# An attention and mixture-of-experts block on one Trainium2 core: the tiled order from pair 2 on, powers on GpSimd, and another split of transfers and scatters

## The chip, the core and the metric

The kernel runs on one core of a Trainium2 chip. The metric is the device time of one execution in microseconds, and the figure compared is the median of several runs. The names of the engines are those of the profile: PE is TensorE (matmuls; PEld is its weight load), DVE is VectorE, ACT is ScalarE, POOL is GpSimd, SP is SyncE, which here only issues transfers. Each engine executes its own instructions in program order. Transfers (DMA) are issued from SP, ACT or POOL.

## What is computed

The input is x with 8 batches of 512 tokens and 256 channels, all in float32. Cut to what matters, the reference is:

```python
xn = layernorm(x)                          # (x - mean) / sqrt(var + 1e-5), per token
# attention, 16 heads of 64, causal
kv = (xn @ w_kv_down) @ w_kv_up            # a latent of rank 128, then keys and values
k, v = kv[..., :1024], kv[..., 1024:]
att = softmax(causal((q @ k^T) * 64 ** -0.5))   # q = xn @ w_q
attn = (att @ v) @ w_out
# feed-forward: 8 experts, the best two per token, and one shared expert
scores = sigmoid(xn @ gate_w.T + lb_bias)
topw, topi = top_k(scores, 2); topw = topw / topw.sum()
for e in range(8):
    sel = (topi == e).any(-1)
    wmean = sum of e's weights / max(number of e's tokens, 1)
    out += where(sel, mlp_e(xn) * wmean, 0)  # mlp: silu(x @ g.T) * (x @ u.T) @ d.T
out += mlp_shared(xn)
result = x + attn + out
```

## The kernel before, in words

**Pairs.** The main loop (L906 and on) runs over 64 steps m, called pairs: 8 batches times 8 pairs of heads. For a pair, TensorE makes `ps_s`, the scores of two heads (`scores`, L615), for four blocks i of 128 query rows, against the 128 (i + 1) keys that causality leaves. VectorE adds the mask and takes the minimum of each row (L622; queries are scaled by a negative number), ScalarE takes the exponent with the row's sum (L629), and VectorE transposes the result in squares of 32 (`transposed`, L642 and L649) into `blk`. Sixteen transfers per pair (`moved`, L661) carry `blk` to `pt` across partitions, so that keys lie on partitions. Two pairs later `weighted` (L704) multiplies `pt` with the values into `ps_y`. The softmax's division comes last: `inverse_sums` (L678 to L683) takes the reciprocals of the row sums, transposes them, and POOL writes them to DRAM as `row`; `spread_sums` (L691) reads `row` back, spread over partitions, as `rb`, in two transfers from SP; ScalarE copies `ps_y` to `yT` (L716), and POOL multiplies it by `rb` (L717). The last pair alone is multiplied by VectorE straight from `ps_y` (L714). `project` (L729) takes the finished batch through `w_out`, with the shared expert's hidden rows.

**Two orders of a pair.** Up to pair 13 (`BLOCK0 = 14`) a pair is done in two halves: blocks (0, 3), then (1, 2), and a half's transposes come behind the next half's scores. From pair 14 on there is one block: scores (3, 1), two exponents, the transposes of block 3, `weighted` of the pair two before, scores (2, 0), two exponents, the transposes of block 1, and then the rest of the list below, at whose 0.65 mark the last transposes, `inverse_sums` and `moved` are emitted. In the old order `moved` of pair m comes at the start of pair m + 1, and `weighted` in the second half of pair m + 2.

**The list of other work.** `put(m, place, f, ...)` notes a piece of work for pair m at a place between 0 and 2; the loop emits a pair's pieces by place. `put_half` counts in half pairs. PE, DVE, ACT and SP keep the order in which instructions are emitted, and so does POOL from pair 0 on. Keys, queries and values of the next pair stand at 0.22 to 0.26.

**Layer norm.** Batch 0 is normalised before the loop (from L816 on: sixteen idle matmuls, then `statistics`, `deviations`, `normalise`, `turn`, then `queries`, `latent`, `keys`). The other batches come in pairs 0 to 10, one every five halves: `load_x` (L135), `statistics` (DVE, L256), `deviations` (DVE, L264 to L273: the reciprocal root by a starting guess on the bits and three Newton steps), `normalise` (POOL, L278), two `turn`s (PE transposes, L288, and an ACT copy), `logits` (L297) and `save_xnT`. In the same pairs POOL issues transfers that fill a DRAM buffer with zeros (L232), lay out the experts' weights (L224) and begin the sums (L244).

**Router, scatter, experts.** The router (L326 to L437) runs in pairs 11 to 13, mostly on VectorE. In pairs 14 to 21 each pair has four `scatter_rows` (L449), each two indirect transfers of 128 rows from POOL, which sort the tokens by expert. In these pairs `moved` gives one of its sixteen transfers to POOL and five to ACT, whose five are kept back until the next pair's block (`rest`); SP issues ten. In other pairs POOL has five and SP eleven. From pair 22 on `expert_fetch`, `expert_turn`, `expert_hidden`, `expert_down` and `expert_add` (L485 to L536) run for 39 tiles of 256 rows, spread over the half pairs up to pair 59.

Of the kernel before, what the change touches and what calls it, by code (L numbers as in the profile page):

```python
# [32 lines left out]
F32 = mybir.dt.float32  # L33
I32 = mybir.dt.int32
# [14 lines left out]
def kernel(  # L49
# [196 lines left out]

    mv = keep.tile([P, NTILE, 2], F32, name="mv")
    rstd = keep.tile([P, NTILE], F32, name="rstd")
    sc = keep.tile([P, NTILE, E], F32, name="sc")
    xnTs: dict = {}  # L250
    lats, qs, ks, vs, pts, rss, rbs, blks = {}, {}, {}, {}, {}, {}, {}, {}
# [4 lines left out]
        nc.vector.bn_stats(st, xins[n // NQ][:, n % NQ, :])  # L256
        nc.vector.bn_aggr(mv[:, n, :], st)

    def deviations(b):


        ve, y, z = (small.tile([P, NQ], F32, tag=f"dev{k}", name="dev") for k in range(3))
        half = small.tile([P, NQ], I32, name="half")
        nc.vector.tensor_scalar_add(ve, mv[:, ts(b, NQ), 1], 1e-5)  # L264
        nc.vector.tensor_single_scalar(half, ve.bitcast(I32), 1, op=ALU.logical_shift_right)
        nc.vector.tensor_scalar(
            y.bitcast(I32), half, -1.0, float(0x5F3759DF), ALU.mult, ALU.add
        )
        for k in range(3):
            nc.vector.tensor_mul(z, y, y)  # L270
            nc.vector.tensor_mul(z, z, ve)
            nc.vector.tensor_scalar(z, z, -0.5, 1.5, ALU.mult, ALU.add)
            nc.vector.tensor_mul(y if k < 2 else rstd[:, ts(b, NQ)], y, z)  # L273

    def normalise(b, by):
        for j in range(NQ):
            n = b * NQ + j
            by.tensor_scalar(  # L278
                xns[:, n, :C], xins[b][:, j, :], mv[:, n, 0:1], rstd[:, n : n + 1],
                ALU.subtract, ALU.mult,  # L280
            )

# [368 lines left out]
                    pr[:, j, nr * P :].rearrange("p (b k) -> p b k", k=QB),  # L651
                )

    def moved(b, p, by_pool, by_act=0):


        pt = ptp.tile([P, NB, 2, NBLK, QB], F32, name="pt")

        def begin(by, k):
            a, kb = divmod(k, NB)  # L660
            by.dma_start(pt[ts(kb, QB), a], blks[b, p][ts(a, QB), kb])  # L661

        left = []
        for k in range(NB * NB):
            if k * by_pool % 16 < by_pool:
                begin(nc.gpsimd, k)
            elif k % 3 == 1 and len(left) < by_act:
                left.append(k)
            else:
                begin(nc.sync, k)  # L670
        pts[b, p] = pt
        return lambda: [begin(nc.scalar, k) for k in left]

    def inverse_sums(b, p):


        ri, riT = ris[p % len(ris)]
        nc.vector.reciprocal(  # L678
            ri[:, : 2 * NQ], rss[b, p].rearrange("p j i -> p (j i)")
        )  # L680
        nc.vector.transpose(riT, ri)  # L681
        row = rowp.tile([NB, QB, QB], F32, name="row")
        nc.gpsimd.dma_start(row.rearrange("a x q -> (a x) q"), riT)  # L683
        rows[b, p] = row

    def spread_sums(b, p):

        rb = rbp.tile([P, NB, NQ * QB], F32, name="rb")
        for j in range(2):
            row = rows[b, p][:, ts(j, NQ), :].rearrange("a i q -> a (i q)")  # L690
            nc.sync.dma_start(  # L691
                rb[ts(j, D)], row.unsqueeze(0).broadcast_to([D, NB, NQ * QB])
            )
        rbs[b, p] = rb

    def weighted(b, p, final=False):


        ps = bank([P, NB, NQ, QB], "ps_y")
        for c in range(NQ):  # L700
            for j in range(2):
                h = 2 * p + j
                at = at_ci[c, c]
                nc.tensor.matmul(  # L704
                    ps[ts(j, D), :, c:, :],
                    vs[b, h // VH][:, c, ts(h % VH, D)],
                    pts[b, p][:, :, j, at : at + NQ - c, :],
                    start=(c == 0), stop=(c == NQ - 1),
                )
        yT = ytp.tile([P, T], F32, name="yT")  # L710
        y = yT.rearrange("p (i a q) -> p a i q", a=NB, q=QB)
        rb = rbs[b, p].rearrange("p a (i q) -> p a i q", q=QB)
        if final:
            nc.vector.tensor_tensor(y, ps, rb, ALU.mult)  # L714
        else:
            nc.scalar.copy(y, ps)  # L716
            nc.gpsimd.tensor_tensor(y, y, rb, ALU.mult)  # L717
        yTs[b, p] = yT
# [42 lines left out]


    EARLY, HALF = 0.3, 0.65
    BLOCK0 = 14
    plan: dict = {}

    def put(m, place, f, *a):
        if place >= 2:
            m, place = m + 1, place - 2
        plan.setdefault(m, []).append((place, len(plan[m]) if m in plan else 0, f, a))  # L770
# [44 lines left out]
    idle = bank([P, T], "ps_i")  # L815
    for k in range(8):  # L816
        nc.tensor.matmul(idle, ones, mask, start=True, stop=True)
    for n in range(NQ):
        statistics(n)
    deviations(0)  # L820
    normalise(0, nc.vector)
    xnTs[0] = xtp.tile([P, NCC, T], F32, name="xnT")
    for h in range(2):
        turn(0, h, xnTs[0])
    queries(0, 0)
    latent(0)
    keys(0, 0)
    put(0, 0.5, lambda: logits(0, xnTs[0]))

# [4 lines left out]
    def put_half(h, place, f, *a):  # L834
        put(h // 2, h % 2 + place, f, *a)
# [5 lines left out]
    for b in range(1, B):  # L841
        h = (b - 1) * LNH // 2
        if b > 2:
            put_half(h - 2, 0.5, load_x, b)
        for j in range(NQ):
            put_half(h + j // 2, 0.6, statistics, b * NQ + j)
        put_half(h + 2, 0.35, deviations, b)
        put_half(h + 2, 0.36, normalise, b, nc.gpsimd)
        put_half(h + 4, 0.1, start_turn, b)
        put_half(h + 5, 0.1, lambda b: turn(b, 1, lnT[b]), b)  # L850
        put_half(h + 6, 0.4, lambda b: (logits(b, lnT[b]), save_xnT(b, lnT[b])), b)
# [19 lines left out]
    for k in range(12):  # L871
        put(R0 + k // 4, 0.35 + 0.5 * (k % 4), lambda: next(steps, None))
    S0 = R0 + 3
    for n in range(NTILE):
        put(S0 + n // NQ, 0.35 + 0.5 * (n % NQ), scatter_rows, n)


    def begin_experts():
# [3 lines left out]
        ep = tmp_pools.enter_context(tc.tile_pool(name="ep", bufs=1))  # L882
        xouts = ep.tile([P, NQ, C], F32, name="xout")

    E0 = S0 + NTILE // NQ
    END = len(pairs) - 5
    put(E0, 0.1, begin_experts)
    first, n_halves = 2 * E0 + 5, 2 * (END - E0) - 7
# [9 lines left out]
        put_half(2 * END + b, 0.7, bring_out, b)  # L898
    put_half(2 * END + B - 1, 0.7, bring_back)

    scattering = range(S0, S0 + NTILE // NQ)
    ordered = ExitStack()
    last = []
    rest = []
    assert BLOCK0 <= S0
    for m in range(len(pairs) + 1):  # L906
        if m == 0:
            ordered.enter_context(tc.manual_schedule(engines={nc.gpsimd.engine}))
        todo = sorted(plan.pop(m, ()), key=lambda e: e[:2])
        for g, group in enumerate(((0, 3), (1, 2)) if m < BLOCK0 else ()):  # L910
            chunks, exps = scores(*pairs[m], group)
            for chunk in last:
                transposed(*chunk)
            last = chunks
            if g == 0 and m > 0:
                moved(*pairs[m - 1], 5)
            for e in exps[:2]:
                e()
            del exps[:2]
            for place, _, f, a in todo:  # L920
                if (place >= 1) == g:
                    if place - g > EARLY:
                        while exps:
                            exps.pop(0)()
                    f(*a)
                    if exps:
                        exps.pop(0)()
            while exps:
                exps.pop(0)()
        if m < BLOCK0:  # L930
            continue

        chunks, exps = [], []
        if m < len(pairs):
            chunks, exps = scores(*pairs[m], (3, 1))
            for chunk in last:
                transposed(*chunk)
            if last:
                moved(*pairs[m - 1], 5)
            last = []  # L940
            exps.pop(0)()
            exps.pop(0)()
            transposed(*chunks.pop(0))
            weighted(*products.pop(m))
            more = scores(*pairs[m], (2, 0))
            exps.pop(0)()
            exps.pop(0)()
            transposed(*chunks.pop(0))
            chunks, exps = more
        for f in rest:  # L950
            f()
        rest = []


        for place, _, f, a in todo + [(2, 0, lambda: None, ())]:
            if place > EARLY - 0.07:
                while exps:
                    exps.pop(0)()
            if place > HALF and chunks:
                while chunks:  # L960
                    transposed(*chunks.pop(0))
                inverse_sums(*pairs[m])
                if m in scattering:
                    rest = [moved(*pairs[m], 1, 5)]
                else:
                    moved(*pairs[m], 8 if m >= len(pairs) - 2 else 5)
            f(*a)
            if exps:
                exps.pop(0)()
# [3 lines left out]
    for tt in range(NQ):  # L973
        project(B - 1, tt, pss[tt], first=NS + NPAIR - 3, last=NS + NPAIR - 1)
    assert not plan and products.keys() == {len(pairs) + 1}, (plan, products)
    weighted(*pairs[-1], final=True)
    for tt in range(NQ):
        project(B - 1, tt, pss[tt], first=NS + NPAIR - 1)
    ordered.close()
# [45 lines left out]
```

## Time and profile before

| | |
|---|---|
| runs, median (lowest to highest) | 987.74 us (986.42 to 988.87), 3 runs |
| the profiled execution | 987.82 us; its span, first to last instruction, 986.1 us |
| mean granted TensorE clock | 0.978 |
| busy in the span | PE 933.2 us (95%), PEld 562.6, DVE 596.4, ACT 506.9, POOL 597.5 |
| transfers | 190.63 MB in 127594 packets; queue q1 (SP) 38.0% of 16 engines' span, q0 (POOL) 34.6% |

A busy share is a mean over stages that have different limits, so the profile is read by stage. "Granted clock" is the share of TensorE's full speed that the throttle gave. In the chain of waits each row is a start in us, a length in us, and the instruction, transfer or wait that held the end back at that moment; a name with q behind the engine (SPq, ACTq) is an instruction of the engine's queue, such as the issue of a transfer. In a timeline, the brackets hold the idle time in front of an instruction and what ended it.

### The profile page before, as it was taken

What the parts mean: (1) busy time and instruction counts of PE and PEld (TensorE: products, weight loads), DVE (VectorE), ACT (ScalarE), POOL (GpSimd) and SP (SyncE); (2) the same over time, 40 slices, a digit from 0 to 9 for tenths busy, and PEclk for the clock granted to TensorE, in tenths of its full rate; (3) what the DMA queues carried; (4) which work ended last, traced back from release to release, by engine and by line L of the source; (5) the groups of instructions that cost most, each with busy time, mean ns of one, the idle gap of its engine ahead of it and who ended that gap; (6) DMA issues with size and microseconds to landing.
All of it is one profiled execution on the core that took longest, in us unless ns stands there. A gap on an engine that the chain in (4) does not pass through costs nothing.

```text
span 986.1 us, 16151 instructions
## 1 busy us (share of the span) xinstructions
PE 933.2 (95%) x4326; PEld 562.6 (57%) x4326; DVE 596.4 (60%) x2160; ACT 506.9 (51%) x1468; POOL 597.5 (61%) x819
## 2 busy tenths in 40 slices
PE   8898999997679889999999999999999999999997
PEld 3454555643346435675666756576556775557555
DVE  3986783796543567446664456754567546674660
ACT  2564464544443456445664556644467544664550
POOL 2587676346677764646676566675757747665450
PEclk9899899999789999999999999999999999999999
DMA  7489788675566768867787677886778868767782
GB/s 263 124 267 307 239 280 279 169 213 170 167 185 165 203 169 227 206 148 160 197 195 204 164 164 190 209 207 157 166 181 209 202 152 193 184 151 155 194 238 79
DMA packets 127594, 190.63 MB, mean 193 GB/s; under 512 B 24896, under 2 KB 88640, under 8 KB 127264
## 3 DMA queue, kind: packets, MB, share of 16 engines
q1 hardware_dynamic: 88160, 104.28, 38.0%
q0 software_dynamic: 36864, 81.78, 34.6%
q10 hardware_dynamic: 2480, 3.55, 1.2%
q8 instruction: 35, 0.57, 0.3%
q14 instruction: 55, 0.45, 0.2%
HBM read 66.45 MB, written 50.18 MB: 118 GB/s over the span
## 4 chain that ended last, share of the span: by engine, by line
PE 76%; DMA 7%; DVE 5%; SPq 4%; ACT 3%; issue 2%; ACTq 1%; POOL 0%; another core or an unknown queue 0%; POOLq 0%; DVEq 0%
PE ps_s L615 14%; PE ps_o L729 13%; PE ps_y L704 13%; PE ps_q L587 9%; PE ps_e L512 7%; PE ps_k L578 5%; PE ps_v L568 4%; SPq L661 4%; PE ps_gu L470 3%; PE ps_ed L525 3%; DMA pt<-blk 3%; ACT pr L629 2%; PE ps_x L500 2%; PE ps_lg L297 1%; DMA rb<-row 1%
## 5 line engine op out<-in xcount | busy, mean ns | idle before, releaser
L622 DVE CUSTOM_DVE_ANT_0 ps_s<-ps_s,mask 128x128 f32<-128x128 f32 (+3 forms) x512 | 241.5, 516 | 207.9 <-PE ps_s L615 155.1
L629 ACT ACTIVATE pr<-ps_s,mn 128x128 f32<-128x128 f32 (+3 forms) x512 | 268.6, 534 | 152.8 <-DVE mn L622 125.7
L642 DVE STREAM_TRANSPOSE blk<-pr 128x384 f32<-128x384 f32 (+2 forms) x512 | 209.5, 449 | 24.6 <-ACT pr L629 15.5
L615 PE MATMUL ps_s<-k,q 64*128 64x512 f32 (+3 forms) x1024 | 189.3, 471 | 30.6 <-ACT q L592 20.8
L661 POOL DMA_DIRECT2D pt<-blk x294 | 156.4, 649 | 71.0 <-DVE ri L678 30.6
L536 POOL DMA_INDIRECT acc_d<-ye,to x78 | 127.5, 1635 | 93.5 <-issue 38.3
L704 PE MATMUL ps_y<-pt,v 128*64 128x512 f32 (+3 forms) x1024 | 157.6, 451 | 8.1 <-DVE th L462 4.2
L615 PEld LDWEIGHTS ps_s<-k,q 64*128 64x128 f32 x1024 | 92.0, 190 | 116.6 <-issue 52.5
L717 POOL TENSOR_TENSOR yT<-yT,rb 128x512 f32<-128x512 f32 x63 | 84.6, 1342 | 96.7 <-ACT yT L716 89.4
L704 PEld LDWEIGHTS ps_y<-pt,v 128*64 128x64 f32 x1024 | 70.2, 140 | 102.8 <-issue 82.9
L729 PE MATMUL ps_o<-wo_sb,yT 128*128 128x256 f32 x512 | 120.1, 380 | 2.3 <-POOL yT L717 1.5
L587 PE MATMUL ps_q<-xnT,wq_sb 128*128 128x512 f32 x256 | 121.0, 595 | 0.7 <-ACT xnT L291 0.7
L729 PEld LDWEIGHTS ps_o<-wo_sb,yT 128*128 128x128 f32 x512 | 96.9, 190 | 17.5 <-POOL yT L717 1.9
L629 ACT ACTIVATION_READ_ACCUMULATOR pr<-ps_s,mn 128x1 f32 x512 | 106.4, 208 | 0.0
L683 POOL DMA_DIRECT2D row<-riT x64 | 46.7, 729 | 58.4 <-DVE riT L681 47.7
L587 PEld LDWEIGHTS ps_q<-xnT,wq_sb 128*128 128x128 f32 x256 | 49.3, 193 | 55.5 <-issue 51.6
L512 PE MATMUL ps_e<-xgT,w 128*128 128x256 f32 x312 | 74.3, 381 | 0.1
L622 DVE DVE_READ_ACCUMULATOR2_ANT mn<- 128x1 f32 x512 | 72.6, 142 | 0.0
L449 POOL DMA_INDIRECT xg_d<-xn,at_i x64 | 62.9, 982 | 13.1 <-issue 13.1
L578 PE MATMUL ps_k<-lat,wkv_sb 128*128 128x512 f32 x128 | 69.8, 628 | 0.7 <-ACT lat L560 0.7
L512 PEld LDWEIGHTS ps_e<-xgT,w 128*128 128x128 f32 x312 | 58.7, 190 | 17.2 <-issue 5.8
L716 ACT COPY yT<-ps_y 128x512 f32<-128x512 f32 x63 | 37.1, 588 | 59.6 <-PE ps_y L704 44.1
(137 smaller groups left out, 1020.0 us busy)
## 6 DMA issues: line engine op xcount, KB each, us to landing
pt<-blk SPq DMA_DIRECT2D x690, 80.0 KB
pt<-blk POOLq DMA_DIRECT2D x294, 80.0 KB
rb<-row SPq DMA_DIRECT2D x128, 128.0 KB
xg_d<-zero POOLq DMA_DIRECT2D x26, 408.0 KB
xg<-xg_d SPq DMA_DIRECT2D x39, 272.0 KB
acc_d<-in_x_dram POOLq DMA_DIRECT2D x8, 512.0 KB
xin<-in_x_dram SPq DMA_DIRECT2D x7, 512.0 KB
xnT_d<-lnT SPq DMA_DIRECT2D x7, 512.0 KB
```

Source lines behind the costliest of these rows:

```text
L512: nc.tensor.matmul(ps[:, v, :], w[:, ds(at + cc * I, I)], turned[t][0][:, cc, :], start=(cc == 0), stop=(cc == NCC - 1),)
L536: nc.gpsimd.indirect_dma_start(out=acc_d[:, :], out_offset=bass.IndirectOffsetOnAxis(ap=turned[t][1][:, u : u + 1], axis=0), in_=results[t ...
L578: nc.tensor.matmul(ps, wkv_sb[:, ts(p, P)], lats[b], start=True, stop=True)
L587: nc.tensor.matmul(ps, wq_sb[:, cc, ts(p, P)], xnTs[b][:, cc, :], start=(cc == 0), stop=(cc == NCC - 1),)
L615: nc.tensor.matmul(pss[j][:, ds(at, n)], q[ts(j, D), ts(i, P)], k[ts(j, D), :n], start=True, stop=True,)
L622: nc.vector.tensor_tensor_reduce(out=pss[j][:, ds(at, n)], in0=pss[j][:, ds(at, n)], in1=mask[:, T - n :], scale=1.0, scalar=NO_MIN, op0=A ...
L629: nc.scalar.activation(o, s, AF.Exp, bias=mn, scale=-1.0, accum_out=rs[:, j, i : i + 1])
L642: nc.vector.transpose(blk[:, :, j, i : i + (nr - 1) * (NQ - 1) + 1 : NQ - 1, :].rearrange("p b c q -> p c b q"), pr[:, j, : nr * P].rearra ...
L661: by.dma_start(pt[ts(kb, QB), a], blks[b, p][ts(a, QB), kb])
L704: nc.tensor.matmul(ps[ts(j, D), :, c:, :], vs[b, h // VH][:, c, ts(h % VH, D)], pts[b, p][:, :, j, at : at + NQ - c, :], start=(c == 0), s ...
L717: nc.gpsimd.tensor_tensor(y, y, rb, ALU.mult)
L729: nc.tensor.matmul(ps, l[:, ts(tt, P)], r, start=(k == 0), stop=(k == len(ops) - 1))
```

## The change

It has six parts.

1. `BLOCK0` goes from 14 to 2: pairs 2 to 13 are emitted in the order that pairs 14 to 63 have already.
2. `deviations` becomes two POOL instructions, an addition and a power with exponent -0.5, in place of fifteen on DVE. `load_x` is placed half a pair earlier.
3. In the scatter pairs ACT issues no transfers: POOL issues two of the sixteen, SP fourteen. VectorE multiplies `ps_y` by `rb` in these pairs, so that ACT's copy and POOL's multiply go.
4. The 32 `scatter_rows` are shared over nine pairs, 14 to 22, as 3, 3, 3, 3, 5, 5, 4, 3, 3. The experts begin a pair later and end where they ended.
5. `row` is laid out so that a head's 512 values lie together, and `rb` comes in one transfer from SP in place of two. The order of its columns changes with it.
6. The prologue takes `deviations` and `normalise` in two halves and computes the latent before the queries.

```diff
+    exponent = const.tile([P, NQ], F32, name="exponent")
+    nc.gpsimd.memset(exponent, -0.5)
...
-    def deviations(b):
...
-        for k in range(3):
-            nc.vector.tensor_mul(z, y, y)
-            nc.vector.tensor_mul(z, z, ve)
-            nc.vector.tensor_scalar(z, z, -0.5, 1.5, ALU.mult, ALU.add)
-            nc.vector.tensor_mul(y if k < 2 else rstd[:, ts(b, NQ)], y, z)
+    def deviations(first, count):
+
+        r = rstd[:, ds(first, count)]
+        nc.gpsimd.tensor_scalar_add(r, mv[:, ds(first, count), 1], 1e-5)
+        nc.gpsimd.tensor_tensor(r, r, exponent[:, :count], ALU.pow)
...
-    def moved(b, p, by_pool, by_act=0):
+    def moved(b, p, by_pool):
...
+        for k in range(NB * NB):
             a, kb = divmod(k, NB)
+            by = nc.gpsimd if k * by_pool % 16 < by_pool else nc.sync
             by.dma_start(pt[ts(kb, QB), a], blks[b, p][ts(a, QB), kb])
...
-        row = rowp.tile([NB, QB, QB], F32, name="row")
-        nc.gpsimd.dma_start(row.rearrange("a x q -> (a x) q"), riT)
+        row = rowp.tile([QB, NB, QB], F32, name="row")
+        nc.gpsimd.dma_start(row.rearrange("x a q -> a x q"), riT)
...
-        rb = rbp.tile([P, NB, NQ * QB], F32, name="rb")
-        for j in range(2):
-            row = rows[b, p][:, ts(j, NQ), :].rearrange("a i q -> a (i q)")
-            nc.sync.dma_start(
-                rb[ts(j, D)], row.unsqueeze(0).broadcast_to([D, NB, NQ * QB])
-            )
+        rb = rbp.tile([P, T], F32, name="rb")
+        row = rows[b, p][: 2 * NQ].rearrange("(j i) a q -> j (i a q)", j=2)
+        nc.sync.dma_start(rb, row.unsqueeze(1).broadcast_to([2, D, T]))
...
-        rb = rbs[b, p].rearrange("p a (i q) -> p a i q", q=QB)
-        if final:
+        rb = rbs[b, p].rearrange("p (i a q) -> p a i q", a=NB, q=QB)
+        if by_vector:
...
-    BLOCK0 = 14
+    BLOCK0 = 2
...
-    for n in range(NQ):
+    for n in range(0, NQ, 2):
         statistics(n)
-    deviations(0)
-    normalise(0, nc.vector)
+        statistics(n + 1)
+        deviations(n, 2)
     xnTs[0] = xtp.tile([P, NCC, T], F32, name="xnT")
     for h in range(2):
+        normalise(2 * h, 2, nc.vector)
         turn(0, h, xnTs[0])
+    latent(0)
     queries(0, 0)
-    latent(0)
...
-            put_half(h - 2, 0.5, load_x, b)
+            put_half(h - 3, 0.5, load_x, b)
...
-    for n in range(NTILE):
-        put(S0 + n // NQ, 0.35 + 0.5 * (n % NQ), scatter_rows, n)
+
+    SHARE = (3, 3, 3, 3, 5, 5, 4, 3, 3)
+    assert sum(SHARE) == NTILE
+    for k, share in enumerate(SHARE):
+        for n in range(share):
+            put(S0 + k, 0.35 + 1.6 / share * n, scatter_rows, sum(SHARE[:k]) + n)
...
-    E0 = S0 + NTILE // NQ
+    E0 = S0 + len(SHARE)
...
-    scattering = range(S0, S0 + NTILE // NQ)
+    scattering = range(S0, E0)
...
-            weighted(*products.pop(m))
+            weighted(*products.pop(m), by_vector=m in scattering)
...
-        for f in rest:
-            f()
-        rest = []
...
-                if m in scattering:
-                    rest = [moved(*pairs[m], 1, 5)]
-                else:
-                    moved(*pairs[m], 8 if m >= len(pairs) - 2 else 5)
+                moved(*pairs[m], 2 if m in scattering else 8 if m >= len(pairs) - 2 else 5)
```

## The prediction

> **What bounds the kernel now.** I read the table of windows first, cut where the stages begin. A pair m is one of the 64 (batch, two heads) steps; its start is its first score matmul (L615) in TensorE's timeline. Columns: window, its length, then busy us (and instructions) of PE, PEld, DVE, ACT and POOL, granted TensorE clock, DMA share, GB/s.
>
> ```profile
> 39.90:149.90 110.00, 104.68 (x506) 57.67 (x506) 88.86 (x378) 59.19 (x176) 82.70 (x105) 0.92 0.86 269
> 149.90:218.50 68.60, 65.50 (x292) 38.47 (x290) 46.72 (x159) 32.16 (x90) 33.96 (x51) 0.98 0.77 224
> ...
> 232.40:280.70 48.30, 30.16 (x129) 14.23 (x128) 23.80 (x87) 19.33 (x62) 35.55 (x61) 0.85 0.65 191
> ...
> 371.80:916.60 544.80, 544.18 (x2616) 348.66 (x2616) 317.25 (x1105) 306.32 (x869) 344.08 (x421) 1.00 0.78 183
> ```
>
> The rows are pairs 2-9, 10-13, 15-17 and 24-59. In the last, over half of the kernel, TensorE is busy 544.18 of 544.80 us at full clock: nothing in this change can shorten it. What can be won lies in the first 372 us, most densely in pairs 15-17, where rows are scattered: 30 of 48 us busy, clock 0.85.
>
> TensorE's timeline gives the pace to hope for. Pairs 60-62 have the tiled block and no extra work:
>
> ```profile
> 916.63 1.56 PE L615 MATMUL ps_s<-k,q 64*128 64x512 f32 x8
> ...
> 925.62 1.56 PE L615 MATMUL ps_s<-k,q 64*128 64x512 f32 x8 [0.42 <-ACT q L592]
> ...
> 934.61 1.56 PE L615 MATMUL ps_s<-k,q 64*128 64x512 f32 x8 [0.42 <-ACT q L592]
> ...
> 265.45 2.29 PE L615 MATMUL ps_s<-k,q 64*128 64x512 f32 x8 [3.89 <-ACT q L592]
> ...
> 280.69 2.08 PE L615 MATMUL ps_s<-k,q 64*128 64x512 f32 x4 [5.02 <-ACT q L592]
> ```
>
> From start to start a bare pair takes 8.99 us; the same pair among the scatters takes 15.24 (265.45 to 280.69), and both end on ScalarE's `q`. The chain of waits says why (start, us, what):
>
> ```profile
> 271.80 0.51 ACTq L661
> 272.32 0.21 ACT pr L629 x2
> 272.53 0.37 ACTq L661
> 272.90 0.09 ACT pr L629
> 272.99 0.12 issue
> 273.11 4.62 DMA pt<-blk
> 277.73 0.02 ACT k L580
> 277.75 0.46 issue
> 278.20 1.94 ACT pr L629 x8
> 280.14 0.50 ACT q L592
> ```
>
> ScalarE's own transfers (L661) stand in its queue from 271.80; its next copy starts at 277.73, after a `pt` transfer has landed. 5.9 us of a 15.24 us pair go there. The matmuls also run slow behind the idle time: `ps_y` takes 3.66 us at 267.74 in the chain and 2.30 at 918.20.
>
> **The change, part by part.** The profiled execution took 987.82 us, its span 986.1; 1.7 us lie around it. The median of the runs is 987.74, so one sum serves for both.
>
> *Prologue.* The turn (L288) starts at 11.85, right behind the idle matmuls, while normalising ends at 10.82: the earlier powers and the half-wise normalising stay hidden behind 1.0 us of cover. The new latent order is on the path: `ps_q` 1.98 and `ps_lat` 1.73 run before ScalarE's `lat` copy 0.59, and keys wait for it. With the latent first, that copy lies under the queries: about -0.9 us.
>
> *Powers on POOL.* DVE's 15 short operations (L264 to L273) stand on the chain from 34.92 to 37.79, 2.9 us in front of pair 2. They leave: -2.9. Two POOL instructions replace them. No row shows a power; the nearest on POOL are 0.28 us (`to`, 128x2) and 1.22 (`xn`, 128x256), so 0.6 to 2.4 us per batch, the value taken 0.6, since four columns are nearer to two than to 256. TensorE needs the result two half pairs later; gone that cover, 7 x 2.4 = 17 us would be the worst.
>
> *Tiled block in pairs 2-9* (110.0 us). By rows at full pace: 8 x 8.99; 13 half turns at 0.45; 6 logits at 1.70; two shared halves at 3.43; one latent 1.72: 71.9 + 5.9 + 10.2 + 6.9 + 1.7 = 96.6. So at most 13.4 are to be had. Several old pairs already run at this pace (pair 4: 14.31 against 8.99 + 0.45 + 1.70 + 3.43 = 14.57), so the block as such wins little. The largest stall is VectorE's 7.3 us for `xin`: SP issues it at 85.75, behind eleven slow `pt` issues, and it lands 6.23 us later. Half a pair earlier (some 6 us) removes nearly all. I take -6.5. Against more speaks the DMA share, 0.86. Against even that: `weighted` moves from the second half of pair m+2 to its front, about 5 us earlier, while 11 issues (0.64 each) and a landing of 2 to 6 us need 9 to 13 us. If that ends last, +0.8 us in each of eight pairs, +6. Bounds -13.4 and +6.
>
> *Pairs 10-14* (68.6 + 13.9). At full pace TensorE needs 62.3 + 10.7 = 73.0. But the router's 57 VectorE operations sum to 20.9 us, beside 7.5 per pair (the mean of pairs 60-62) and 1.4 for a shared half: pairs 11-14 hold 53.6 us for VectorE against 53.1 for TensorE, in 58.2 now. VectorE becomes co-bound. -4 for all five, between 0 and -9.5.
>
> *Scatter, pairs 15-22* (232.4 to 361.2, 128.8 us). Removed: five ScalarE issues per pair and its `y` copy (0.59), POOL's multiply (1.34). Added: one VectorE multiply (0.69, L714), which starts when `ps_y` ends, while VectorE waits for the next scores (in pairs 60-62 the first mask starts 1.1 us after `ps_y`), so it is hidden; gone that cover, 0.69 x 9 = 6. SP gets 14 of 16 transfers, up from 10: 14 x 0.635 + 0.66 for `rb` = 9.6 us per pair, more than 8.99. The last `pt` and `rb` land some 13 us after `blk` is ready (8.9 of issue, 4.6 the landing in the chain); `weighted` and the multiply of two pairs later want them at 1.9 and 4.2 us into their pair. At 8.99 they would be late by 2 to 3; at 10.5 nearly in time. POOL with three tiles: 6 x 1.29 + 0.73 + 2 x 0.65 = 9.8, under 10.5. So bare pairs 10.5, between 8.99 and 12.5 (issues at their mean of 0.667, every landing late). With 17.13 for a pair with projections, 12.42 for one with a shared half and 10.71 with a latent, the sum is 3 x 10.5 + 2 x 17.13 + 2 x 12.42 + 10.71 = 101.3: -27. At worst the pairs without projection stay near what they are: 115, -14.
>
> Behind a short wait the clock also keeps up. In pairs 15-17 the slower matmuls cost 2.8 us per pair (`ps_s` 2.93 for 1.49, `ps_y` 3.66 for 2.30); that is inside the -27. The Trainium skill, TensorE: Matmul & The Clock Gate (section on the HAM clock gate), lets the clock halve after an idle window of about 3.4 us. By that rule, waits of 2 to 3 us in the new pairs would cost no clock, and the 101.3 would stand even at the late end of the landings.
>
> *Pair 23 and the experts.* 10.63 becomes about 9.6: -1. Experts start a pair later in a stage that TensorE fills; their work is the same: 0.
>
> *`rb` as one transfer.* One issue of 0.63 to 0.66 less on SP per pair (counted), and pieces of 2 KB for 512 B. Its source has an outermost count of 2. Every transfer in this trace has 16 or more there (each of SP's 899 carries sixteen semaphore packets), so its spread is not to be read off: either 16 engines as now, or no more than 2. I take 16, the form of every row.
>
> Sum: 987.8 - 0.9 - 2.9 - 6.5 - 4 - 27 - 1 = 945.5, say **946**.
>
> **Rivals.**
> *Thin gain.* SP and the landings take ScalarE's place: the scatter stage at its bad end (-14), pairs 2-14 unchanged, the prologue kept (-3.8): **970**. For it: a DMA share of 0.86 in pairs 2-9, old pairs already at pace. Against it: 5.9 us that leave each bare scatter pair.
> *The early stages give it back:* the block wins nothing in pairs 2-9 and waits for `pt` (+6), the powers cost 0.6 of their worst (+10), scatter is at its bad end (-14), the prologue kept (-3.8): about **986**, no change.
> *Slower: two DMA engines.* If `rb` goes over two engines, each carries 64 packets of 2 KB per pair. Such packets took 86 ns on average (384 in the trace): 5.5 us per pair, 352 in all. An engine is now busy 74.3% of 986 = 733 us (the page's queues: 38.0, 34.6, 1.2, 0.3, 0.2), of which 69 are `rb`'s. The two would need 733 - 69 + 352 = 1016 us, and every `pt` waits for them: about **1025**. From four engines on (664 + 176 = 840) it would not bind. Before the trace of after, only the count of 2 speaks for it; that 2 KB rows are read at all speaks for a shorter transfer.
> The Trainium skill, DMA: Bandwidth & Descriptors (section "Why a DMA increments its semaphore by 16 and not by 1"), speaks for the slow case. It says that the engines number at most 16 and must divide the slowest dimension of both sides, which here makes two. By that rule the sum would be 1025 and not 946; no row of this trace has a slowest dimension under 16 to test it.
>
> **How the numbers follow.** Forecast 0.56 (928, all stages at full pace, to 960), thin gain 0.20, no change 0.04, two engines 0.20. What the measurement can tell from no change is about 0.3%, 3 us. Faster 0.76, same 0.04, slower 0.20. The range leaves out the slow case alone: 925 to 992.
>
> **What would show it.** Right: bare scatter pairs near 10.5 us with no ACTq on the chain; pair 2 starting near 36; VectorE's wait for `xin` gone; pairs 24-59 unchanged. Wrong: `rb` landing later than its 4.8 us of now (median from first issue), 14 SP issues spread over more than 10 us, TensorE waiting for `pt` or `rb` in pairs 24-59 (two engines), or `weighted` waiting for `pt` in pairs 2-9.

## The result and the profile after

The changed kernel takes **1116.6 us** (median of 4 runs, 1105.7 to 1118.9) beside 988.3 us for the kernel before in the same comparison: ratio 1.1285, 95% interval 1.1232 to 1.1337. The forecast was 946 us, the range 925 to 992. The direction was wrong. The rival on that side, two DMA engines for `rb`, had a chance of 0.20 and a price of 1025.

The same four stages as in the first view of before, in the table of windows of after (same columns):

```profile
36.48:174.69 138.21, 105.95 (x505) 60.11 (x505) 78.33 (x289) 61.56 (x182) 101.00 (x130) 0.88 0.75 227
174.69:251.77 77.08, 67.53 (x291) 40.91 (x290) 45.87 (x163) 32.35 (x91) 31.01 (x44) 0.93 0.67 192
269.75:314.71 44.96, 30.66 (x127) 14.28 (x126) 24.50 (x85) 17.57 (x58) 23.30 (x42) 0.85 0.53 156
420.22:1024.70 604.48, 560.81 (x2616) 357.77 (x2617) 318.61 (x1105) 306.12 (x869) 347.51 (x416) 0.97 0.70 163
```

Pairs 2-9 took 110.0 before and take 138.2; pairs 10-13 went from 68.6 to 77.1; pairs 15-17, where most was to be won, from 48.3 to 45.0 (three tiles a pair in place of four); and pairs 24-59, which nothing was to touch, from 544.8 to 604.5. The bytes are the same (190.71 MB for 190.63), and the GB/s fell in every stage.

The waits of SP's queue name the largest difference (line waited for by which transfer: us, times, longest). First before, then after:

```profile
SPq L691 <- DMA row<-riT: 31.2, 17, 4.5
...
SPq L661 <- DMA rb<-row: 5.3, 7, 2.0
```

```profile
SPq L651 <- DMA rb<-row: 203.6, 47, 7.2
SPq L651 <- DVE blk L633: 121.2, 24, 11.5
SPq L670 <- DMA row<-riT: 98.4, 26, 10.4
```

SP's issues of `pt` now wait 203.6 us for `rb` to land, where they waited 5.3. In the trace SP's 870 transfers share eight semaphores: an issue takes over the semaphore of a transfer some eight places ahead and waits until that one has landed, so a slow transfer stops SP's queue. The kernel's end shows it bare (chain of waits of after: start, us, what):

```profile
1036.44 12.73 DMA rb<-row
...
1052.98 12.54 DMA rb<-row
...
1069.32 12.94 DMA rb<-row
...
1084.16 13.71 DMA rb<-row
```

That `rb` went over two engines can be counted in the trace. I read the 4-byte packets on SP's queue as semaphore steps, one for each engine that carries a part of a transfer. Before has 14384 of them, 899 transfers times 16. After has 13024 for 870 transfers, which is 806 times 16 and 64 times 2. Of `rb`'s 2 KB packets one or two run at a time for 94% of their time, and never more than four; with `rb` in two transfers (`a_rb_two`, below) up to twenty do. From issue to last packet `rb` takes 9.2 us (median), where it took 4.8. The Trainium skill, DMA: Bandwidth & Descriptors, in its section "Why a DMA increments its semaphore by 16 and not by 1", has the rule that the engines must divide the slowest dimension of both sides; the count agrees.

SP's `pt` transfers, which go over all sixteen engines, are held up with it. Of the sixteen semaphore steps of a `pt` transfer the last two come 2.2 us after the fourteenth (median of the 430 whose steps are all in the trace), where they came 0.2 us after it before; from the end of its issue a `pt` takes 5.4 us to land in place of 2.8. In `a_rb_two` these are 0.2 and 2.6 again.

### The profile page after: what moved, and what is told of

Same layout as the page of the kernel before. It is cut to its first block, busy times and chain, and to the rows that moved or that the text cites. A ratio compares the mean times of both kernels' runs of the same rounds, so it can differ in the third digit from the quotient of the medians.

```text
span 1113.2 us, 15995 instructions
## 1 busy us (share of the span) xinstructions
PE 965.0 (87%) x4326; PEld 581.9 (52%) x4326; DVE 585.2 (53%) x2049; ACT 502.2 (45%) x1459; POOL 610.2 (55%) x834
## 2 busy tenths in 40 slices
DMA packets 101016, 190.71 MB, mean 171 GB/s; under 512 B 23744, under 2 KB 53696, under 8 KB 100688
## 5 line engine op out<-in xcount | busy, mean ns | idle before, releaser
L681 PE MATMUL ps_y<-pt,v 128*64 128x512 f32 (+3 forms) x1024 | 184.0, 509 | 96.1 <-DMA pt<-blk 68.2
L606 PE MATMUL ps_s<-k,q 64*128 64x384 f32 (+3 forms) x1024 | 190.4, 481 | 31.5 <-ACT q L583 23.0
L681 PEld LDWEIGHTS ps_y<-pt,v 128*64 128x64 f32 x1024 | 82.8, 157 | 204.2 <-issue 157.4
L651 POOL DMA_DIRECT2D pt<-blk x299 | 161.5, 703 | 33.3 <-DVE ri L658 24.1
L606 PEld LDWEIGHTS ps_s<-k,q 64*128 64x128 f32 x1024 | 96.3, 198 | 125.1 <-issue 68.8
L694 POOL TENSOR_TENSOR yT<-yT,rb 128x512 f32<-128x512 f32 x54 | 78.2, 1448 | 100.7 <-DMA rb<-row 59.0
L578 PE MATMUL ps_q<-xnT,wq_sb 128*128 128x512 f32 x256 | 123.8, 607 | 0.0
L663 POOL DMA_DIRECT2D row<-riT x64 | 61.0, 952 | 99.7 <-DVE riT L661 73.9
L693 ACT COPY yT<-ps_y 128x512 f32<-128x512 f32 x54 | 31.6, 585 | 162.1 <-PE ps_y L681 147.6
L440 POOL DMA_INDIRECT xg_d<-xn,at_i x64 | 62.9, 983 | 13.3 <-issue 13.3
L571 ACT COPY k<-ps_k 128x512 f32<-128x512 f32 x64 | 37.5, 585 | 72.3 <-remote 40.7
```

The source lines that it names most:

```text
L578: nc.tensor.matmul(ps, wq_sb[:, cc, ts(p, P)], xnTs[b][:, cc, :], start=(cc == 0), stop=(cc == NCC - 1),)
L606: nc.tensor.matmul(pss[j][:, ds(at, n)], q[ts(j, D), ts(i, P)], k[ts(j, D), :n], start=True, stop=True,)
L681: nc.tensor.matmul(ps[ts(j, D), :, c:, :], vs[b, h // VH][:, c, ts(h % VH, D)], pts[b, p][:, :, j, at : at + NQ - c, :], start=(c == 0), s ...
```

## The experiments

All ratios are to the kernel before, run on the same chip. On the chips of the first sixteen kernels before takes 988 to 992 us; on those of the last two (`e_best`, `d_break2`) it takes 968 and 966, and that turned out to matter.

### First question: how much is `rb`, and why

`a_rb_two` is the change with `rb` in two transfers, one per head, so that 64 partitions are outermost; the layout and the 2 KB pieces stay:

```diff
-        row = rows[b, p][: 2 * NQ].rearrange("(j i) a q -> j (i a q)", j=2)
-        nc.sync.dma_start(rb, row.unsqueeze(1).broadcast_to([2, D, T]))
+        for j in range(2):
+            row = rows[b, p][ts(j, NQ)].rearrange("i a q -> (i a q)")
+            nc.sync.dma_start(rb[ts(j, D)], row.unsqueeze(0).broadcast_to([D, T]))
```

> The changed kernel with rb in two transfers, one per head with 64 as the outermost count, from the new row layout (pieces of 2 KB). Theory (one rb transfer runs on two DMA engines, lands in 9.2 us for 4.8, and SP's queue waits for it, 203.6 us in all): the time falls from 1117 to 940-960 us and SP's wait for rb to under 15 us. Rival (the tiled block in pairs 2 to 13 and the fuller SP queue cost the time): it stays above 1050.

1012.8 us, 1.0206 (1.0130 to 1.0282). Its line in SP's waits is back to

```profile
SPq L651 <- DMA rb<-row: 2.0, 3, 0.9
```

So the one transfer costs 104 us. The forecast for the rest, 940 to 960, is missed by over 50: a second loss of some 20 us is left.

`b_rb_one` is before with part 5 alone (the diff of `row` and `rb` as in the change).

> The kernel before with part 5 alone: the new row layout and rb in one transfer. Theory (two engines): 1080-1120 us, with pairs 24-59 longer by 40 us or more. Rival (the other parts cost the time): 983-993 us.

1080.0 us, 1.0917 (1.0847 to 1.0987), SP waiting 185.4 us for `rb`: 88.5 of the 104 us without the other parts. `a_rb_old` is the change with part 5 undone wholly (the lines of before).

> The changed kernel with part 5 undone as a whole: old row layout, two rb transfers of 512 B pieces. Theory (two engines): 940-960 us, within 5 us of the kernel with two transfers of 2 KB pieces. If the size of the pieces counts by itself: over 5 us slower than that kernel.

1015.6 us, 1.0265 (1.0201 to 1.0328): as `a_rb_two`. Layout and piece size are worth nothing that these runs can tell. `a_rb_quarter` keeps the one transfer with 2 outermost, but carries a quarter of its bytes; left out are three quarters of the row sums (all query blocks are divided by those of block 0):

```diff
-        rb = rbp.tile([P, T], F32, name="rb")
-        row = rows[b, p][: 2 * NQ].rearrange("(j i) a q -> j (i a q)", j=2)
...
+        rb = rbp.tile([P, P], F32, name="rb")
+        row = rows[b, p][: 2 * NQ].rearrange("(j i) a q -> j i (a q)", j=2)[:, 0]
...
```

> The changed kernel with rb still in one transfer with outermost count 2, but a quarter of its bytes (64 KB, pieces of 512 B). It leaves out three quarters of the row sums: every query block is divided by the sums of block 0. If the bytes on two engines are the cost (64 x 27 ns = 2 us per pair in place of 5.5): 940-970 us. If a transfer on two engines costs by being one, whatever its bytes: above 1050.

1008.3 us, 1.0174 (1.0098 to 1.0249), SP's wait 5.8 us. Two engines cost nothing that can be told when they have little to carry. Whether the whole `rb` hurts because it lands late, in a queue that waits for it, or because the two engines are full, this run does not part: it ends both. An estimate speaks for engines that are nearly full. The times of `rb`'s packets, halved, and a sixteenth of those of all others add up to 1095 us of a span of 1113 in after, and to 812 of 1006 here. The trace names no packet's engine, so this takes the others to be spread evenly.

### Second question: where the other 20 us are

From here on `a_rb_two` is the base, and parts are put back. By its pairs it starts pair 2 at 37.27 (before 39.90), and then loses: pairs 2-9 114.1 us (110.0), 10-13 72.3 (68.6), 14 17.5 (13.9), 15-22 142.7 (128.8), 23 13.3 (10.6); pairs 24-59 546.5 (544.8). These are readings of one trace each, uncertain by some us: pairs 10-13 take 68.6 us in before's trace and 64.0 to 65.1 in those of `b_direct`, `b_spread16` and `b_spread12`, which have the same code up to there.

`c_block14`:

```diff
-    BLOCK0 = 2
+    BLOCK0 = 14
```

> Base: a_rb_two, whose pairs 2 to 14 took 203.9 us where before took 192.5 (110.0, 68.6 and 13.9). Here only the first pair of the tiled block goes back from 2 to 14. Theory (the tiled block in the early pairs costs time): pairs 2 to 14 take about 193 and the kernel 999 to 1004 us. Rival (the tiled block gains there, as predicted, and the powers on GpSimd are what costs): pairs 2 to 14 get no shorter, 1012 to 1024 us.

997.2 us, 0.9979 (0.9928 to 1.0031): 15.6 us less than `a_rb_two` on the same chip. In its trace pairs 2-9 take 112.1 us in place of 114.1, pairs 10-14 78.3 in place of 89.9, and pairs 15-22 138.3 in place of 142.7. Pair 4 shows the wait that the block brings. Its chain in `a_rb_two`, from 9 us ahead of `ps_y` on:

```profile
64.84 1.34 SPq L651
66.19 0.04 issue
66.23 1.75 SPq L651
67.98 0.05 issue
68.03 0.03 SPq L671
68.06 0.04 issue
68.10 5.41 DMA rb<-row
73.51 0.04 issue
73.55 4.28 PE ps_y L682 x16
```

The same pair in `c_block14`:

```profile
73.64 1.28 PE ps_s L606 x8
74.92 0.58 PE ps_t L279 x4
75.50 0.87 PE ps_v L559 x4
76.37 2.30 PE ps_y L682 x16
```

In the block `ps_y` stands near the front of its pair, right behind SP's issues of `pt` (here 1.3 and 1.8 us each) and their landing; the pair takes 22.6 us. (The chain names `rb`, which `ps_y` does not read. It reads `pt`, whose last issue ends at 67.98; `rb` only takes over semaphores that `pt` transfers had before it.) In the old order `ps_y` comes last, everything has long landed, and the pair takes 14.3.

Pair 4 is not the whole of it: other pairs of 2-9 give nearly all of its 8.3 us back, and what pairs 10-14 wait for, where most is lost, is not shown here. That they lose is: over all traces of kernels with `rb` in two transfers or a quarter of it they take 85 to 93 us in the eleven with the block from pair 2, and 78 to 83 in the seven with the block from pair 14.

`b_block2`, before with `BLOCK0 = 2` alone, asks whether the block needs the other parts for that.

> Before (988.6 us) with the tiled block from pair 2 on, and nothing else of the change. Theory (the block multiplies the weights near the front of a pair and so waits there for the spread sums of the pair before, with or without the powers on GpSimd): 996 to 1006 us. Rival (the block is slow only beside the powers on GpSimd): 982 to 991 us.

1018.1 us, 1.0276 (1.0220 to 1.0332): it does not. Alone it costs more than I expected, pairs 2-9 taking 125.2 us.

`b_powers` is before with parts 2 and 6 (powers, prologue, earlier `load_x`).

> Before (988.3 us) with the powers on GpSimd, the new prologue and the earlier loads of x, and nothing else of the change. Theory (this part gains what the start of pair 2 shows, 37.27 against 39.90 us): 984 to 987 us, the gain within the prologue. Rival (GpSimd, which also does the normalisation and issues transfers, is late in pairs 2 to 14 because of the powers): 988 to 995 us.

991.9 us, 1.0012 (0.9975 to 1.0049). Pair 2 starts at 35.85, so the gain is there; by the end it cannot be told from none.

`c_scatter_old` puts all of the scatter part back (parts 3 and 4 as before).

> Base: a_rb_two (the change with rb in two transfers), 1012.8 us, whose pairs 15 to 23 took 156.0 us where before took 139.4. Here the scatter pairs are those of before: ScalarE's five transfers, one of sixteen on GpSimd, the copy on ScalarE and the multiply on GpSimd, four tiles in each of eight pairs. Theory (the scatter part itself loses): pairs 15 to 23 fall back to about 140 and the kernel takes 994 to 999 us. Rival (the scatter pairs are slow because of something that other parts do to them, or of the clock): they stay near 150 and the kernel at 1008 or more.

1002.8 us, 1.0112 (1.0073 to 1.0150): 10 us less than `a_rb_two`, and above my 994 to 999. Put back one by one: the shares alone (`c_uniform`, four tiles in each of eight pairs),

> Base: a_rb_two, 1012.8 us; of its scatter part only the shares go back: four tiles in each of eight pairs in place of 3, 3, 3, 3, 5, 5, 4, 3, 3 in nine. Theory (a pair with indirect scatters loses some 5 us whatever their number, since TensorE's signals come late in it): one scatter pair fewer and no pair with five tiles, 1001 to 1007 us, all or most of what c_scatter_old got back. Rival (the removed transfers of ScalarE or the multiply on VectorE lost it): 1010 us or more.

1009.9 us, 1.0226 (1.0180 to 1.0272), no gain; ScalarE's transfers alone (`c_act_moves`),

> Base: a_rb_two, 1012.8 us; of its scatter part only ScalarE's five transfers a pair go back (GpSimd one of sixteen, SyncE ten). Theory (the scatter pairs wait for TensorE's late signals, not for ScalarE): within 5 us of a_rb_two, 1008 to 1018. Rival (SyncE's queue of 14 transfers a pair is what made them longer): 1000 to 1006 us.

1010.6 us, 1.0211 (1.0175 to 1.0247), none either; and the multiply alone:

```diff
-            weighted(*products.pop(m), by_vector=m in scattering)
+            weighted(*products.pop(m))
```

> Base: a_rb_two, 1012.8 us; of its scatter part only the multiply goes back (copied by ScalarE, multiplied by GpSimd, in the scatter pairs). Theory (VectorE, waiting in order for TensorE's late signal ahead of its multiply, holds up the masks and transposes behind it; with the shares, 3 us, and ScalarE's transfers, 2 us, undone singly, about 5 of the 10 us that all three cost are left for it): 1005 to 1009 us. Rival (the three cost nothing singly, only together): 1010 to 1015 us.

986.7 us, **0.9966** (0.9940 to 0.9992). I had expected 5 us and it gave 26 (on another chip than `a_rb_two`, where before takes the same time; by the ratios 24). With the multiply back on ScalarE and GpSimd, and ScalarE's transfers still gone, pairs 15-22 take 112.6 us in place of 142.7, and 128.8 before. So moving the multiply to VectorE cost more than the whole scatter part, and taking ScalarE's transfers away (with the shares) gained: 1.0112 against 0.9966.

### Third question: what the scatter pairs wait for

In `a_rb_two` ScalarE stands idle with its work apparently ready. Three rows of its timelines (TensorE, ScalarE, GpSimd):

```profile
261.57 1.12 PE L569 MATMUL ps_k<-lat,wkv_sb 128*128 128x512 f32 x2
```

```profile
267.60 0.59 ACT L571 COPY k<-ps_k 128x512 f32<-128x512 f32 x1 [7.01 <-remote]
```

```profile
262.29 0.97 POOL L440 DMA_INDIRECT xg_d<-xn,at_i  x1 [0.19 <-issue]
263.25 0.12 POOL L448 MEMSET between<- 128x1 f32 x1
263.56 0.97 POOL L440 DMA_INDIRECT xg_d<-xn,at_i  x1 [0.19 <-issue]
```

`ps_k` ends at 262.69, and the copy of it starts 4.9 us later; the profile names no engine of this core as releaser, only "remote". The mean of this gap over pairs 15 to 24 is 3.9 us in `a_rb_two` and 3.7 in before, where ScalarE's own issues are a part of it. What the stage has in both kernels, and others lack, is GpSimd's train of indirect scatters, so `d_scatter_direct` issues plain transfers in their place:

```diff
-            ins = nc.gpsimd.indirect_dma_start(
-                out=xg_d[:, :],
-                out_offset=bass.IndirectOffsetOnAxis(ap=at_i[:, k, n : n + 1], axis=0),
-                in_=xns[:, n, :],
-                in_offset=None,
-            )
+            ins = nc.gpsimd.dma_start(xg_d[ts(TOPK * n + k, P), :], xns[:, n, :])
```

> Base: a_rb_two, 1012.8 us. In its scatter pairs ScalarE and VectorE start up to 8 us after TensorE's records of what they wait for have ended (pair 18: ps_k ends at 278.9, the copy of k starts at 283.5), which no other stage shows. Here each scatter is a plain transfer of the same 128 rows to fixed rows, issued by GpSimd in the same place; left out: the rows don't go to their experts' slots, so the experts work on other rows. Theory (the indirect transfers hold up TensorE's signals, by their instruction or their many descriptors): the late starts are gone, the pairs 15 to 23 take about 115 us in place of 156, the kernel 968 to 980 us. Rival 1 (the bytes of the transfers do it): no difference, 1005 to 1015 us. Rival 2 (the late starts are TensorE at work that the records don't show): no difference either, and the late starts stay where TensorE has been idle.

974.5 us, 0.9824 (0.9748 to 0.9899). The same rows:

```profile
242.76 1.12 PE L564 MATMUL ps_k<-lat,wkv_sb 128*128 128x512 f32 x2
```

```profile
243.93 0.59 ACT L566 COPY k<-ps_k 128x512 f32<-128x512 f32 x1 [1.65 <-PE ps_k L564]
```

The copy starts 0.05 us behind the matmul, and a bare pair takes 8.98 us, as it does in pairs 60-62. Two windows, pair 16 of `a_rb_two` and then of this kernel:

```profile
255.26:270.56 15.30, 10.02 (x43) 4.81 (x43) 8.62 (x31) 5.75 (x20) 8.40 (x15) 0.83 0.56 159
```

```profile
246.88:255.86 8.98, 8.57 (x42) 4.25 (x42) 8.13 (x30) 5.74 (x20) 5.31 (x15) 1.00 0.79 233
```

The bytes are the same and flow faster. GpSimd's time is left as a rival: a plain transfer takes it 0.54 us, an indirect one 0.97. `d_direct_slow` follows each plain transfer with six small memsets in place of one:

> Base: d_scatter_direct, 974.5 us, whose plain transfers also took GpSimd less time (0.54 against 0.97 us each). Here six small memsets follow each of them in place of one, so that GpSimd is busy about as long for a tile as with the indirect ones. Left out as there: the rows don't go to their experts' slots. Theory (the indirect form itself holds up TensorE's signals): k is copied within 0.7 us of the end of its matmul in every pair, pairs 15 to 22 take 100 to 106 us, the kernel 970 to 980. Rival (it is GpSimd's time, and what queues behind it): pairs 15 to 22 take 125 us or more, the kernel 995 or more.

981.7 us, 0.9887 (0.9830 to 0.9944), 2 us over my range, pairs 15-22 in 99.9 us. GpSimd now takes 1.6 us from one transfer to the next, more than the 1.28 of the indirect ones, and every copy of `k` starts on time:

```profile
251.47 0.54 POOL L440 DMA_DIRECT2D xg_d<-xn  x1
252.00 0.90 POOL L444 MEMSET between<- 128x1 f32 x6
253.04 0.54 POOL L440 DMA_DIRECT2D xg_d<-xn  x1
```

On these chips it is the indirect form, not the bytes and not GpSimd's time. `b_direct` does the same exchange in before:

> Before (991.4 us on this chip) with plain transfers to fixed rows in place of the indirect scatters, and nothing of the change; left out: the rows don't go to their experts' slots. Theory (what holds the scatter pairs is the indirect transfers, not the transfers that ScalarE issues, which stay here): pairs 15 to 22 take 100 to 108 us in place of 128.8, the kernel 958 to 972. Rival (d_scatter_direct was short because ScalarE issues nothing there): pairs 15 to 22 take 115 us or more, the kernel 978 or more.

970.0 us, 0.9811 (0.9775 to 0.9847), pairs 15-22 in 113.7 us, missing my 100 to 108. Its pairs 16 and 17 take 13.9 and 13.8 us, where `d_scatter_direct`, with no transfers on ScalarE, has 8.98 and 10.5. (The two also differ in the multiply, the shares and the block.) ScalarE's rows in pair 17, of before and then of `b_direct`:

```profile
273.11 1.99 ACTq L661 DMA_DIRECT2D pt<-blk  x3
277.72 0.59 ACT L580 COPY k<-ps_k 128x512 f32<-128x512 f32 x1 [4.74 <-DMA pt<-blk]
```

```profile
267.70 2.22 ACTq L656 DMA_DIRECT2D pt<-blk  x3
269.97 0.58 ACT L575 COPY k<-ps_k 128x512 f32<-128x512 f32 x1 [2.42 <-PE ps_q L582]
```

With plain transfers the copy of `k` starts right behind ScalarE's last issue (within 0.05 us in six of the eight pairs 15-22); in before it does so in three, and in the other five it starts 2.0 to 4.2 us later. So both stories were true of before: its scatter pairs paid for the indirect form and for ScalarE's transfers. In `a_rb_two` the same transfers, put back, cost nothing (`c_act_moves`).

Does the loss go by pair or by tile? `b_spread16` (before with two tiles in each of sixteen pairs) and `b_spread12` (2, 2, 2, 4, 4, 3, 3, 2, 2, 2, 2, 4).

> Before (991.4 us) with two tiles' scatters in each of sixteen pairs in place of four in each of eight; the experts start eight pairs later. Theory (loss per pair with scatters, whatever their number): eight more pairs lose some 4 us each, 1010 to 1030 us. Rival (loss per scatter, or only while GpSimd has no gap between them): no difference or a gain, 970 to 992 us.

> Before (988.6 us), its 32 tiles' scatters shared over twelve pairs: 2, 2, 2, 4, 4, 3, 3, 2, 2, 2, 2, 4, the most where TensorE has 17 us of work or more in the pair, so that late signals cost nothing there. From b_spread16: two tiles in a bare pair cost 2 to 3 us of idle TensorE, four in a long pair none; its loss came later, where the experts had eight pairs fewer. Theory (loss by tile in a bare pair, 1.4 us each; 20 tiles in bare pairs in place of 24): 980 to 988 us. Rival (the experts squeezed into four pairs fewer lose more than that): 990 to 1002 us.

1012.7 us, 1.0226 (1.0184 to 1.0267), and 995.0, 1.0016 (0.9977 to 1.0056). The first landed where the loss by pair put it, but for another reason: its scatter pairs were shorter (pairs 15-22 108.4 us), and what it lost came in pairs 24-59, 591.5 us, where the experts are squeezed. The second gained 15 us in pairs 15-22 and lost 26 in 24-59. The loss goes rather by tile, and spreading has no net gain.

### Two last runs

`e_best` is the change with `rb` in two transfers, the multiply back, and `BLOCK0 = 14`.

> The change with three parts taken back: rb in two transfers, the multiply of the scatter pairs on ScalarE and GpSimd again, the tiled block from pair 14 on. From c_multiply_old, 986.7 us, less what c_block14 got back on a_rb_two (15 us): 972 us. Theory (the parts add up, since they act in different stages): 967 to 977 us, faster than before and than the change. Rival (what the block loses early is made up by the scatter stage's waiting): 980 to 990 us.

961.0 us where before takes 968.1: **0.9926** (0.9901 to 0.9951). It is faster than both kernels, by less than the parts promised. `d_break2` keeps VectorE's multiply and has GpSimd add zero to its output at the place of the old multiply:

```diff
             nc.vector.tensor_tensor(y, ps, rb, ALU.mult)
+            if p != NPAIR - 1 or b != B - 1:
+                nc.gpsimd.tensor_scalar_add(yT, yT, 0.0)
```

> Base: a_rb_two, 1012.8 us (1.0206 of before), whose multiply in the scatter pairs is VectorE's. It stays there; added is a pass of GpSimd that adds zero to its output, so that nothing changes, placed where GpSimd's multiply was; it waits for VectorE and so parts the scatters as the multiply did in c_multiply_old (986.7 us, 0.9966 of before). Every multiply on VectorE gets it but the kernel's last. Theory (an unbroken train of indirect scatters holds up TensorE's signals, and a GpSimd operation in its middle lets them through): 0.993 to 1.008 of before, pairs 15 to 22 in 113 to 124 us, in place of 142.7. Rival (VectorE, waiting in order for TensorE ahead of its multiply, holds up the masks behind it): 1.017 of before or more, pairs 15 to 22 in 135 us or more.

1.0058 (1.0029 to 1.0087), pairs 15-22 in 99.4 us, which would suit the theory. I do not count it for that. In this run every copy of `k` is on time, also behind three scatters that nothing parts. Rows of GpSimd, TensorE and ScalarE:

```profile
256.72 1.04 POOL L440 DMA_INDIRECT xg_d<-xn,at_i  x1 [0.30 <-issue]
257.77 0.11 POOL L448 MEMSET between<- 128x1 f32 x1
258.06 0.99 POOL L440 DMA_INDIRECT xg_d<-xn,at_i  x1 [0.18 <-issue]
259.06 0.11 POOL L448 MEMSET between<- 128x1 f32 x1
259.36 0.96 POOL L440 DMA_INDIRECT xg_d<-xn,at_i  x1 [0.19 <-issue]
```

```profile
258.62 1.13 PE L569 MATMUL ps_k<-lat,wkv_sb 128*128 128x512 f32 x2
```

```profile
259.79 0.59 ACT L571 COPY k<-ps_k 128x512 f32<-128x512 f32 x1 [1.65 <-PE ps_k L569]
```

`e_best` shows the same, and both ran on the chips where before is 20 us faster. It seems that on these two chips indirect scatters do not make TensorE's results late. No trace of before or of `a_rb_two` on them exists, so that is an inference; that before takes there about what `b_direct` takes on the others (970.0) fits it. What `d_break2` was to tell stays open.

## Why the prediction was wrong

**`rb` as one transfer** is the step that failed most: "I take 16, the form of every row". It was two engines, 104 of the 128 us. The rows proved nothing: none had fewer than 16 outermost. The rival had the right mechanism, "every `pt` waits for them", and too small a price, 1025: it took 86 ns for a packet of `rb` and 664 us for the rest, where after shows 98 ns and 693 us, and with these its own sum gives 1095 us. It left out SP, which in order waits for each `rb` to land (203.6 us), with the `pt` transfers behind it. How much each of the two adds is not parted.

**Scatter pairs, -27.** In `a_rb_two` they lost 14. Two terms failed. The first is the reading of the chain, "5.9 us of a 15.24 us pair" for ScalarE's transfers. Part of it was theirs: the last of their issues ends at 275.10 (273.11 + 1.99). The 2.6 us from there to 277.72 were a result of TensorE that came late under indirect scatters, and are gone in `b_direct`; the chain put `DMA pt<-blk` over them, and I believed it. The second is "one VectorE multiply (0.69) ... hidden; gone that cover, 0.69 x 9 = 6": it cost 24 to 26 us. A step can cost what it makes others wait, and that has no bound in its own duration. Without that multiply the bare pairs come near the forecast, 11.1, 11.9 and 10.6 us (`c_multiply_old`; said 10.5), but the stage takes 112.6, near its bad end of 115 (said 101.3).

Why the multiply on VectorE costs so much is not settled. Either VectorE waits in order for TensorE's late result ahead of the masks, or the old multiply parted GpSimd's train of scatters and let results through. For the second speaks that the mean gap of `k` falls from 3.9 to 1.9 us in `c_multiply_old`; neither was shown. That the multiply is free where results are on time is shown: `d_scatter_direct` has it, at 8.98 us in two of its three bare pairs.

**Tiled block, -6.5 and -4.** In `a_rb_two` it was +4.1 in pairs 2-9 and +7.3 in 10-14; undone, -15.6 in all. The first lies inside its bounds (-13.4 to +6), the second outside (0 to -9.5): the sentence "If that ends last" named the wait and I priced it only for pairs 2-9. In pair 4 it ended last; what ended last in pairs 10-14 is open. The gain forecast from the earlier `load_x` did come, in pair 5 (21.8 us before, 14.4 in `a_rb_two`, 15.9 in `b_powers`), and other pairs gave it back.

**Prologue and powers, -3.8.** Pair 2 starts 3.4 us earlier in after: right in place and size. That it lasts to the end is not shown (`b_powers`, 1.0012). The power and its addition take GpSimd 0.98 and 0.25 us a batch, twice the 0.6 that I took.

**Pair 23 and the experts, -1 and 0.** Pair 23 was slower, by 2.7 us in `a_rb_two`. The experts' stage was unchanged, as said, once `rb` is apart (546.5 against 544.8).

**The clock.** The forecast that waits of 2 to 3 us cost none does not hold in general. In `c_multiply_old` (timeline and windows):

```profile
250.59 1.56 PE L606 MATMUL ps_s<-k,q 64*128 64x512 f32 x8 [2.49 <-ACT q L583]
262.52 1.82 PE L606 MATMUL ps_s<-k,q 64*128 64x512 f32 x8 [3.36 <-ACT pr L620]
```

```profile
250.59:262.52 11.93, 8.57 (x42) 4.25 (x42) 7.88 (x29) 6.34 (x21) 9.74 (x18) 1.00 0.69 200
262.52:273.15 10.63, 10.21 (x43) 4.62 (x43) 7.65 (x29) 6.34 (x21) 7.92 (x13) 0.84 0.68 192
```

Behind 2.49 us of idle time the pair runs at clock 1.00, behind 3.36 at 0.84. But pair 23 of before stands behind 2.83 us, and has 0.84 as well:

```profile
361.16 2.42 PE L615 MATMUL ps_s<-k,q 64*128 64x512 f32 x8 [2.83 <-ACT q L592]
```

```profile
361.16:371.79 10.63, 10.21 (x42) 4.70 (x42) 7.65 (x29) 6.83 (x22) 6.43 (x9) 0.84 0.75 193
```

Over ten of the traces the mean clock in the 4 us behind a wait of TensorE was under 0.95 in 9 of 14 cases of 2.5 to 3.0 us, and in 10 of 10 of 3.0 to 3.3. The Trainium skill, TensorE: Matmul & The Clock Gate (section on the HAM clock gate), puts the idle window at about 3.4 us. The 3.36 us lie next to it; the shorter waits that cost clock here do not follow from it.

## What to carry to other kernels

Before merging transfers, look at the outermost count of the merged one. Then price it by what each engine that is left must carry and by what waits for it to land, in the issuing queue and on those engines: the bytes in all were the same here, and a quarter of them cost nothing. When an engine idles in one stage alone, exchange what only that stage does before believing the named releaser: plain transfers in place of indirect ones settled here what the chain of waits had misnamed. And undo the parts of a change singly and together: here the multiply hid what the rest of the scatter part gained.

## What the hardware showed that I had not expected

On three chips (before 988 to 992 us), while GpSimd issued indirect scatters of 128 rows every 1.28 us, ScalarE's copies of `k` started on average 3.9 us, at most 7.9, after the recorded end of the matmul (`a_rb_two`, pairs 15 to 24; on the other two chips 4.5 in `c_uniform` and 1.9 in `c_multiply_old`). With plain transfers of the same bytes, and none issued by ScalarE, it was 0.1. Whether TensorE's signal is held up, or its work, which the records then would not show, the runs do not tell. On two other chips (966 and 968) the gap did not appear in two kernels with indirect scatters. A transfer with 2 outermost went over two engines, 64 of 64 times, and the `pt` transfers, which have a share on all sixteen, landed 5.4 us after their issue in place of 2.8.
